# A new order of instructions for the ends of a two-layer graph kernel on one core

## The chip, the cores and the metric

The kernel runs on one core of one Trainium2 chip. The metric is the device time of one execution in microseconds (us), as the median of several runs. A profiled execution gives, besides, the span from its first to its last instruction and what each engine did in it. The engines are called PE (TensorE, matrix products), PEld (its weight loads), DVE (VectorE), ACT (ScalarE), POOL (GpSimd) and SP (SyncE, which here only issues DMAs).

## The reference

There are 128 blocks x[b] of 128 nodes by 512 features in fp32, and one 128x128 matrix adj for all of them. Two layers follow each other, each with a residual and a layer norm:

```
# layer 0, per block
A = adj @ x                       # 128x512
rm = max over features of relu(A + (A + b0 - A))  -> relu(row maximum of A + b0)
x = layernorm(x + rm)
# layer 1, per block: attention with 8 heads of 64, masked by adj == 0
q, k, v = split(x @ w_qkv)
o = (softmax(mask(q k^T / 8)) @ v) @ w_proj + b_proj
x = layernorm(x + o + layernorm(o) * gamma + beta)
```

The layer-0 line is the reference's pairwise maximum as the kernel computes it: a row maximum of adj @ x, a bias and a relu.

## The kernel before

The 128 blocks are taken in 32 groups of 4. Each group needs, per block, some 60 steps, and a step is one short function that issues a few instructions on one engine. The names of the steps are used below with the block in brackets; dm, dd, main and rest carry (group, j) instead, where j is 0 to 3 for the v product of a block and 4 to 11 for a q or k product of the whole group.

- Layer 0: load (SP) brings x; conv (PE, L633) multiplies by adj; cmax (DVE) takes the row maximum; bn and ba (DVE) or add0 and sq0 (ACT) take the moments; relu, rstdx and shiftx or rstd0 and shift0 (POOL) make scale and shift; norm0 (ACT, L705) applies them.
- The transposes of x. In group 0 tx (PE) transposes into PSUM and copy (L767) keeps a plain copy of blocks 0 and 1 for pv, a plain fp32 product with w_v (PE, L778). In every other group xpl (ACT, L717) splits x into 16-bit planes, xrow (SP, L721) writes them to DRAM, and xcross (SP) reads them back with a transposing DMA. There is one buffer of planes, so xpl of the next block waits until xrow of the last one has landed.
- The dense products are done in three reduced-precision terms. xmask, xsub (DVE, L740 and L756), xhigh and xd split x into a high part, a low part and a difference; wmask, wsub, wd, wh, wl do the same for the weights once, at the start. dm (PE, L818 and L819) does the first two terms, dd (PE, L824) the third; main (ACT, L843) and rest (DVE, L847) bring the sums to SBUF.
- Attention: S (PE, L864), masked and rmax (DVE), exps (ACT, L903), recip and wts (DVE), pln (ACT, L918), row (SP) and cross (SP), which turn the weights through DRAM as above, and AV (PE, L950). In the last group T (PE) transposes instead.
- The end of a block: omask, osub (L968), ohigh, od; po and pod (PE) multiply by w_proj; pmain, prest; res, resx, resb, reso bring the residual; sq1 to norm2 are the two layer norms; out writes the block.

The order is not written as loops. Every step of every block has a place, a number, in a table: STEADY for the groups in the middle, one period of 55.2952 apart, FIRST for groups 0 and 1, LAST for groups 30 and 31, SETUP for the weights and constants. group_plan turns the tables into a list, the list is sorted by place, and the steps are issued in that order (L1168) under a manual schedule: each engine gets its own instructions in exactly the order of the list and runs them one after the other. Only the order of the numbers matters; a number is no time. The semaphore waits follow from which step writes and reads what.

HOMES says for every tile which buffer of its kind it gets. ps_1 has four PSUM banks (0 to 3), shared by pa, ptx, pv, pm, pd, pav and the projection; ps_2 has two double ones. A step that fills a bank waits until the last reader of its former content is done. TWO says which of two engines does a step.

Of the kernel before, what the change touches and what calls it, by code (L numbers as in the profile page):

```python
# [88 lines left out]
        'load': [-901.563, -922.473, -922.478, -903.511],  # L89
        'conv': [-846.813, -915.390, -915.506, -874.949],  # L90
        'cmax': [-801.056, -837.693, -879.384, -830.372],
        'relu': [-769.981, -826.342, -869.061, -825.870],
        'bn': [-827.199, -893.843, -914.944, -858.378],
        'ba': [-823.944, -891.308, -906.541, -834.612],
        'rstdx': [-769.986, -871.005, -872.145, -809.784],
        'shiftx': [-756.335, -825.941, -839.332, -806.691],
        'norm0': [-665.371, -805.806, -813.036, -780.621],
        'tx': [-662.290, -792.690, -793.199, -771.754],
        'copy': [-659.866, -737.960],
        'pv': [-512.869, -504.297],  # L100
        'keep': [-512.082, -498.844],
        'xmask': [-660.833, -762.731, -727.868, -730.418],
        'xsub': [-655.987, -732.262, -663.602, -697.023],
        'xhigh': [-645.543, -744.320, -688.080, -657.593],
        'xd': [-624.486, -628.830, -550.270, -602.581],
        'dm': [None, None, -189.208, -190.809, -355.594, -484.251, -628.419, -495.437, -360.548, -512.270, -635.612, -488.644],
        'dd': [None, None, -190.217, -261.030, -354.973, -354.971, -354.968, -468.964, -372.501, -463.622, -459.178, -466.650],
        'main': [None, None, -144.321, -142.898, -350.075, -443.584, -557.996, -457.187, -355.005, -412.729, -587.560, -356.783],
        'rest': [None, None, -132.175, -85.246, -308.148, -283.698, -281.357, -403.261, -319.558, -356.677, -395.445, -311.676],
        'S': [-228.655, -246.003, -152.387, -143.350],  # L110
        'masked': [-207.282, -245.809, -138.500, -87.105],
        'rmax': [-204.167, -238.589, -110.297, -72.325],
        'exps': [-143.767, -228.331, -64.342, -39.835],
        'recip': [-128.447, -159.497, -59.854, -1.024],
        'wts': [-76.979, -133.784, -57.083, 1.778],
        'pln': [-56.268, -102.763, -26.594, 25.922],
        'row': [12.450, -89.665, 22.867, 38.411],
        'cross': [23.073, -54.738, 39.078, 53.987],
        'AV': [41.632, 32.084, 48.580, 62.020],
        'omask': [43.060, 38.063, 55.696, 69.240],  # L120
        'osub': [50.071, 41.766, 56.572, 73.080],
        'ohigh': [46.187, 42.319, 57.889, 94.260],
        'od': [55.963, 50.919, 66.754, 105.184],
        'po': [50.422, 45.682, 70.630, 106.044],
        'pod': [57.744, 53.653, 71.635, 105.297],
        'pmain': [53.386, 50.289, 72.129, 108.935],
        'prest': [61.548, 57.007, 81.360, 111.396],
        'res': [20.431, -449.833, 74.707, 77.734],
        'resx': [65.326, -238.611, 92.577, 103.188],
        'resb': [65.601, 62.299, 100.889, 111.137],  # L130
        'reso': [85.510, 64.948, 103.433, 114.117],
        'sq1': [69.604, 71.004, 98.646, 116.521],
        'sm1': [90.258, 64.542, 94.296, 111.885],
        'st1': [82.652, 85.464, 101.831, 117.141],
        'n1a': [90.344, 80.143, 105.417, 118.025],
        'n1b': [91.956, 89.155, 106.494, 119.198],
        'sq2': [93.227, 93.375, 115.421, 123.874],
        'sm2': [97.804, 89.471, 109.477, 120.474],
        'st2': [101.770, 106.617, 116.322, 126.682],
        'norm2': [102.343, 107.816, 117.180, 127.450],  # L140
        'out': [109.060, 121.436, 120.171, 128.392],
    },
    {
        'load': [-905.274, -696.140, -858.109, -902.178],
        'conv': [-792.111, -663.812, -712.708, -716.977],
        'cmax': [-709.318, -638.776, -690.493, -706.940],
        'relu': [-555.739, None, -616.445],
        'bn': [-703.706, -646.917],
        'ba': [-690.726, -645.927],
        'rstdx': [-558.088],  # L150
        'shiftx': [-554.898],
        'add0': [None, None, -601.344, -604.764],
        'sq0': [None, None, -567.298, -573.370],
        'rstd0': [None, None, -552.984],
        'shift0': [None, None, -518.997],
        'norm0': [-554.884, -502.496, -403.722, -417.718],
        'xpl': [-554.429, -502.196, -391.703, -416.776],
        'xrow': [-470.076, -375.192, -293.759, -319.091],
        'xcross': [-394.778, -319.316, -286.162, -305.221],
        'xmask': [-372.466, -307.177, -249.613, -262.305],  # L160
        'xsub': [-329.385, -262.572, -243.199, -244.783],
        'xhigh': [-275.237, -298.028, -199.736, -215.316],
        'xd': [-272.386, -204.299, -156.069, -159.106],
        'dm': [-10.436, 6.699, -0.683, -0.556, -143.277, -131.813, -122.870, -130.336, -39.992, -105.000, -112.136, -140.915],
        'dd': [-4.815, 6.730, 10.987, 18.045, -127.490, -108.574, -116.018, -118.700, -24.016, -29.807, -26.705, -118.919],
        'main': [1.177, 46.859, 5.350, 6.474, -132.881, -131.684, -115.120, -114.444, -37.456, -88.207, -40.875, -105.235],
        'rest': [1.965, 48.653, 18.540, 20.009, -121.662, -87.519, -102.746, -111.824, -17.484, -23.344, -19.627, -52.332],
        'S': [-11.079, -17.443, -16.256, -1.509],
        'masked': [-10.554, -17.005, -9.812, 6.626],
        'rmax': [-5.380, -16.675, 5.417, 19.372],  # L170
        'exps': [-2.148, -10.618, 7.233, 22.858],
        'recip': [0.765, -9.571, 18.704, 35.680],
        'wts': [6.167, -4.226, 43.122, 35.837],
        'pln': [6.770, 3.285, 56.604, 44.172],
        'row': [16.487, 7.371, 56.843, 54.372],
        'cross': [20.475, 25.543, 61.651, 64.066],
        'AV': [52.512, 52.150, 68.373, 68.094],
        'omask': [63.494, 57.640, 72.391, 77.549],
        'osub': [65.657, 58.241, 79.421, 99.342],
        'ohigh': [65.260, 57.805, 75.915, 100.961],  # L180
        'od': [73.704, 59.905, 88.130, 103.708],
        'po': [69.517, 61.895, 86.954, 104.135],
        'pod': [76.042, 63.614, 93.677, 111.272],
        'pmain': [74.426, 66.789, 96.190, 114.037],
        'prest': [78.300, 68.797, 99.841, 114.042],
        'res': [60.118, 65.341, 97.902, 93.885],
        'resx': [69.088, 68.611, 98.642, 103.374],
        'resb': [72.493, 73.045, 103.649, 115.231],
        'reso': [89.889, 83.803, 109.798, 129.413],
        'sq1': [81.258, 68.947, 107.075, 118.043],  # L190
        'sm1': [86.719, 87.045, 108.620, 116.281],
        'st1': [92.581, 80.193, 119.323, 125.369],
        'n1a': [91.249, 88.810, 118.652, 131.743],
        'n1b': [92.613, 88.815, 123.900, 132.261],
        'sq2': [96.351, 99.085, 124.215, 132.381],
        'sm2': [97.859, 94.858, 125.503, 145.539],
        'st2': [103.342, 102.489, 128.234, 147.699],
        'norm2': [106.369, 103.393, 130.775, 147.977],
        'out': [115.175, 111.613, 147.933, 149.596],
# [28 lines left out]
        'S': [28.905, 28.062, 51.236, 50.349],  # L228
        'masked': [35.272, 37.129, 54.944, 52.529],
        'rmax': [38.080, 38.174, 96.293, 53.051],  # L230
        'exps': [43.345, 51.622, 115.258, 64.145],
        'recip': [49.538, 54.728, 141.791, 70.564],
        'wts': [52.585, 60.636, 147.678, 82.495],
        'pln': [53.581, 61.741, 154.283, 105.933],
        'row': [56.112, 76.901, 159.668, 153.223],
        'cross': [81.989, 84.562, 182.868, 153.372],
        'AV': [85.872, 91.909, 188.022, 153.844],
        'omask': [106.182, 104.214, 188.234, 161.077],
        'osub': [154.777, 106.177, 189.068, 161.598],
        'ohigh': [152.931, 109.298, 193.692, 166.063],  # L240
        'od': [160.331, 144.311, 199.215, 178.233],
# [955 lines left out]
```

## Time and profile before

| | |
|---|---|
| time, median of 3 runs | 1821.26 us (1821.16 to 1822.58) |
| the profiled execution's own time | 1820.26 us |
| its span, first to last instruction | 1818.5 us |
| matrix products on PE | 10525, busy 1791.8 us |
| DVE / ACT / POOL busy | 1584.7 / 1543.2 / 1246.7 us |
| granted TensorE clock, mean | 0.997 |
| DMA | 303.94 MB, of 16 engines the main queue takes 62.9% |

PE has one program, so its idle time can be listed gap by gap from its timeline. In us from the start of the span:

| PE starts again at | idle before it | instruction |
|---|---|---|
| 3.74 | 3.74 | adjT_ps, waits for adj |
| 4.57 | 0.38 | first conv |
| 11.20 | 0.52 | tx(1) |
| 13.79 | 1.94 | tx(3) |
| 16.12 | 0.81 | tx(0) |
| 18.47 | 1.72 | conv(7) |
| 102.74 | 0.95 | dm(1,2) |
| 163.96, 172.02, 177.77, 179.16 | 0.14, 0.17, 0.06, 0.29 | groups 2 and 3 |
| 234.95 | 1.83 | conv(21) |
| 280 to 1680, 8 places | 0.03 to 0.80 each | |
| after the last product, at 1807.7 | 10.8 | the last block's layer norms and its output |

A line of the profile's groups, waits or timeline has the start, the length, the engine, the source line, the operation, what it writes and reads, and in brackets the idle time of the engine just before it with what ended that idle time. "issue" stands where the profile shows nothing that was waited for. Ends of matmuls are modelled; the distance from one start to the next is the better measure (0.227 us for a 128x512 product of the reduced kind).

### The profile page before, as it was taken

How to read it: one execution, taken by the hardware profiler on the slowest of the kernel's cores; microseconds unless marked ns; L12 is line 12 of the kernel's file. 1: busy time of each engine (PE TensorE's matmuls, PEld its weight loads, DVE VectorE, ACT ScalarE, POOL GpSimd, SP SyncE). 2: the span in 40 equal slices, each digit the busy share in tenths (PEclk: the TensorE clock that was granted, in tenths of full speed). 3: DMA queues.
4: the chain of work that ended last, by engine and by line, in shares of the span. 5: the costliest groups of instructions: out<-in, count | busy, mean ns of one | idle time of the engine just before them, and what ended most of it. 6: DMA issues, size and time to landing. Idle time of an engine off the chain costs nothing.

```text
span 1818.5 us, 32498 instructions
## 1 busy us (share of the span) xinstructions
PE 1791.8 (99%) x10525; PEld 1428.0 (79%) x10525; DVE 1584.7 (87%) x2575; ACT 1543.2 (85%) x3959; POOL 1246.7 (69%) x1892
## 2 busy tenths in 40 slices
PE   7999999999999999999999999999999999999997
PEld 4777878888887878887888888888878878877885
DVE  7988888988888988889888888888888988889887
ACT  6987888888888888888889888888888888888786
POOL 5256577666776767776667867667766678668867
PEclk9999999999999999999999999999999999999999
DMA  5666666666666676665767655766567766567543
GB/s 154 159 149 173 161 176 160 155 186 184 161 171 156 168 190 167 183 165 155 186 180 169 162 171 159 198 164 184 163 148 184 180 173 184 154 167 186 169 133 99
DMA packets 486714, 303.94 MB, mean 167 GB/s; under 512 B 399504, under 2 KB 403728, under 8 KB 486544
## 3 DMA queue, kind: packets, MB, share of 16 engines
q1 hardware_dynamic: 485680, 300.75, 62.9%
q8 instruction: 83, 1.36, 0.3%
q10 hardware_dynamic: 864, 1.12, 0.2%
q14 instruction: 87, 0.71, 0.1%
HBM read 73.20 MB, written 131.07 MB: 112 GB/s over the span
## 4 chain that ended last, share of the span: by engine, by line
PE 89%; ACT 5%; DVE 2%; DMA 2%; POOL 1%; issue 1%; SPq 0%; ACTq 0%; POOLq 0%; DVEq 0%
PE psc L864 7%; PE pav L950 6%; PE pa L633 5%; ACT e L903 1%; ACT squares L1063 1%; DMA rows<-planes 1%; ACT planes L918 1%; DMA eT<-rows 1%; DMA rowsx<-xplanes 1%; ACT xplanes L717 0%; PE pv L778 0%; ACT qkT L843 0%; ACT o L1105 0%; POOL sum L1069 0%; ACT xt L705 0%
## 5 line engine op out<-in xcount | busy, mean ns | idle before, releaser
L903 ACT ACTIVATE e<-e,nmax 128x128 f32<-128x128 f32 x1016 | 392.7, 393 | 4.6 <-DVE nmax L886 4.6
L918 ACT COPY planes<-e 128x2048 uint16<-128x2048 uint16 x124 | 235.3, 1897 | 63.3 <-DMA rows<-planes 39.9
L1069 POOL TENSOR_TENSOR sum<-sum,mhalf 128x1 f32<-128x1 f32 (+1 forms) x287 | 195.8, 682 | 23.9
L1063 ACT ACTIVATE squares<-o,sum 128x512 uint8<-128x512 f32 x256 | 182.6, 715 | 18.3 <-DVE o L1056 14.9
L903 ACT ACTIVATION_READ_ACCUMULATOR e<-e,nmax 128x1 f32 x1016 | 195.9, 193 | 0.0
L1072 POOL TENSOR_SCALAR sum<-sum 128x1 f32<-128x1 f32 x256 | 74.9, 294 | 172.3 <-DVE o L1056 169.1
L912 DVE TENSOR_TENSOR e<-e,sums 128x1024 f32<-128x1024 f32 x128 | 182.8, 1445 | 1.9
L1053 POOL TENSOR_TENSOR xb<-xb,o 128x512 f32<-128x512 f32 x124 | 176.7, 1434 | 9.5 <-DVE o L1056 4.9
L1068 POOL TENSOR_SCALAR sum<-sum 128x1 f32<-128x1 f32 (+1 forms) x287 | 103.3, 360 | 114.7 <-ACT squares L1063 96.9
L1044 POOL TENSOR_TENSOR xb<-xb,beta_sb 128x512 f32<-128x512 f32 x124 | 162.7, 1312 | 7.3
L717 ACT COPY xplanes<-xt 128x1024 uint16<-128x1024 uint16 x124 | 129.3, 1043 | 41.1 <-DMA rowsx<-xplanes 40.9
L878 DVE SCALAR_TENSOR_TENSOR e<-psc,mask 128x1024 f32<-128x1024 f32 x127 | 152.0, 1217 | 1.0 <-PE psc L864 0.8
L886 DVE TENSOR_REDUCE nmax<-e 128x8 f32<-128x1024 f32 x127 | 150.9, 1206 | 0.1
L750 POOL TENSOR_TENSOR x_d<-x_h,x_l 128x512 fp32r<-128x512 f32 x97 | 129.2, 1333 | 14.0 <-DVE x_l L756 5.6
L864 PEld LDWEIGHTS psc<-qkT 64*128 64x128 f32 x2048 | 119.5, 188 | 18.3 <-issue 15.3
L864 PE MATMUL psc<-qkT 64*128 64x128 f32 x2048 | 132.1, 279 | 0.0
L633 PE MATMUL pa<-xt,adjT 128*128 128x512 f32 x256 | 125.2, 608 | 4.0 <-DVE ol L968 1.8
L950 PE MATMUL pav<-eT,v 128*64 128x128 f32 x2048 | 126.7, 276 | 1.1 <-DMA eT<-rows 1.1
L950 PEld LDWEIGHTS pav<-eT,v 128*64 128x64 f32 x2048 | 110.5, 137 | 18.2 <-issue 12.7
L1105 ACT ACTIVATE o<-o,sum 128x512 f32<-128x512 f32 x128 | 103.7, 810 | 9.5 <-POOL sum L1101 9.4
L649 POOL TENSOR_SCALAR rm<-rm,b_sb 128x2 f32<-128x2 f32 (+1 forms) x66 | 21.5, 326 | 131.4 <-DVE rm L644 130.9
L1084 DVE SCALAR_TENSOR_TENSOR o<-o,sum,gamma_sb 128x512 f32<-128x512 f32 x128 | 102.8, 803 | 9.3 <-POOL sum L1072 4.9
(4264 smaller groups left out, 5596.6 us busy)
## 6 DMA issues: line engine op xcount, KB each, us to landing
rows<-planes SPq DMA_DIRECT2D x124, 512.0 KB, 4.1
xt<-in_x_dram SPq DMA_DIRECT2D x128, 256.0 KB, 3.4
xb<-in_x_dram SPq DMA_DIRECT2D x128, 256.0 KB, 3.7
out_dram<-o SPq DMA_DIRECT2D x128, 256.0 KB, 2.8
rowsx<-xplanes SPq DMA_DIRECT2D x124, 256.0 KB, 3.4
wraw<-in_L_gnn_w_qkv_dram SPq DMA_DIRECT2D x8, 256.0 KB, 3.9
xT<-rowsx SPq DMA_TRANSPOSE x124, 3.7
eT<-rows SPq DMA_TRANSPOSE x124, 4.6
```

The source lines that it names most:

```text
L633: nc.tensor.matmul(pa[b], adjT, xs[b], start=True, stop=True)
L864: nc.tensor.matmul(psc[:, s, hp, :], qkT[hs, hp, i, :], qkT[hs, KC + hp, i, :], start=not with_mask, stop=not with_mask or hp == HP - 1,)
L878: nc.vector.scalar_tensor_tensor(es[b], pscs.pop(b).rearrange("p s a m -> p (s a) m"), scale, mask_b, op0=ALU.mult, op1=ALU.add,)
L886: nc.vector.tensor_reduce(nmaxs[b], es[b], AX.X, ALU.max, negate=True)
L903: nc.scalar.activation(es[b][:, j, :], src[:, j, :], AF.Exp, bias=nmax[:, j : j + 1], scale=by, accum_out=sums[b][:, j : j + 1],)
L912: nc.vector.tensor_tensor(es[b], es[b], sums.pop(b)[:, :, None].to_broadcast([P, H, P]), op=ALU.mult,)
L918: nc.scalar.copy(pl, es.pop(b).rearrange("p h m -> p (h m)").bitcast(U16).rearrange("p (m s) -> p s m", s=2),)
L950: nc.tensor.matmul(pavs[b][s * HD : (s + 1) * HD, hp, :], v[:, h * HD : (h + 1) * HD], eT[:, s * HP + hp, :], start=True, stop=True,)
L1044: nc.gpsimd.tensor_tensor(xbs[b], xbs[b], beta_sb, op=ALU.add)
L1053: engine.tensor_tensor(xbs[b], xbs[b], os[b], op=ALU.add)
L1063: nc.scalar.activation(junk[:, turn[0], :], src, AF.Square, bias=s[:, 0:1], scale=-float(D), accum_out=s[:, 1:2],)
L1069: nc.gpsimd.tensor_tensor(s, s, mhalf[:, :n], op=ALU.pow)
```

## The change

Only the tables FIRST, LAST, SETUP and HOMES are changed; the code, STEADY and TWO are the same. Every number of FIRST and of SETUP is new, and many of LAST. Since a number acts only through the order, the change is best read as the order on each engine that comes out:

| engine | steps | whose position differs | from | to |
|---|---|---|---|---|
| PE | 1411 | 82 | the 4th | the 154th (pod(7)) |
| ACT | 1657 | 165 | the 2nd | the 225th |
| DVE | 2317 | 234 | the 5th | the 305th, and one more pair |
| POOL | 1273 | 101 | the 2nd | the 130th |
| SP | 899 | 78 | the 3rd | the 116th |

The one pair near the end of DVE is osub(123) and n1b(121), which change places. Nothing else of the last two groups is in another order. After some 240 us of the time before, all engines have the old order.

The first steps, before and after:

```
PE   before adjT conv(2) conv(1) conv(3) conv(0) tx(2) tx(1) tx(3) conv(4) tx(0) conv(7) conv(6) dm(0,10) dm(0,6) conv(5) pv(0) dm(0,9) pv(1) dm(0,7)
     after  adjT conv(2) conv(1) conv(0) conv(3) tx(2) tx(1) tx(3) conv(7) tx(0) conv(6) conv(4) dm(0,10) dm(0,6) conv(5) pv(1) pv(0) dm(0,11) dm(0,7)
DVE  before adjc bn(2) ba(2) bn(1) ba(1) cmax(2) bn(3) wmask6 mask cmax(1) ba(3) cmax(3) bn(0) wsub6 ba(0) wmask10 wd6 cmax(0) xmask(1) wsub10 xsub(1) wd10 xmask(3) xmask(2) xsub(3) xsub(2) xmask(0) copy(0) xsub(0)
     after  adjc bn(2) ba(2) bn(1) cmax(2) bn(0) ba(1) mask bn(3) cmax(1) ba(0) ba(3) wmask6 cmax(0) cmax(3) wsub6 wmask10 wd6 wsub10 xmask(1) wd10 xsub(1) xmask(2) xmask(3) xsub(2) xsub(3) cmax(7) xmask(0) xsub(0)
ACT  before norm0(2) wh6 norm0(1) wl6 norm0(3) xhigh(1) wh10 copy(1) norm0(0) xhigh(3) wl10 xhigh(0) main(0,10) wh9 wl9 main(0,6)
     after  norm0(2) norm0(1) wl6 wh6 wh10 norm0(3) copy(1) xhigh(1) wl10 norm0(0) xhigh(3) xhigh(0) add0(6) main(0,10) sq0(6) wl11 add0(7) wh11 main(0,6)
SP   before load(2) load(1) load(3) lw6 load(0) lw10 lw9 load(4) load(7) load(6) lw11 load(5) lw7
     after  load(2) load(1) load(0) load(3) lw6 lw10 lw5 load(7) lw11 load(6) load(4) lw9 gammb load(5) lw7
```

Further on, around the first attention blocks:

```
PE   before AV(1) S(5) S(6) AV(0) S(4) dm(1,0) po(1) AV(2) po(0) dd(1,0) pod(1) S(7) dm(1,2) dm(1,3) pod(0)
     after  AV(1) S(5) AV(0) S(4) S(6) dm(1,0) dd(1,3) po(1) dm(1,3) dd(1,0) pod(1) S(7) AV(2) dd(1,2) po(0) pod(0) conv(14) conv(15) dm(1,1) dm(1,2)
ACT  before xpl(8) ohigh(1) wl12 exps(5) xpl(9) ohigh(0) norm0(10) exps(4) xpl(10) main(1,0)
     after  xpl(8) pln(3) ohigh(1) xpl(9) main(1,0) exps(5) main(1,3) norm0(10) ohigh(0) xpl(10) exps(4)
SP   before row(1) lw13 cross(1) load(11) load(10) row(0) load(8) load(9) res(0) row(2) cross(0) gamma row(3) cross(2) xrow(8) xcross(8) load(15) xrow(9) cross(3) xcross(9) load(14) xrow(10)
     after  row(1) res(0) load(11) load(10) load(8) row(0) load(9) cross(0) cross(1) row(2) gamma cross(2) xrow(8) row(3) xcross(8) load(15) xrow(9) xcross(9) load(14) xrow(10) cross(3)
```

The core of the diff that makes these orders, cut to lines that are spoken of:

```diff
 FIRST = [
     {
-        'xsub': [-655.987, -732.262, -663.602, -697.023],
-        'copy': [-659.866, -737.960],
+        'xsub': [-1083.930, -1180.700, -1122.347, -1118.864],
+        'copy': [-1043.146, -1134.306],
...
     {
-        'main': [1.177, 46.859, 5.350, 6.474, -132.881, -131.684, -115.120, -114.444, -37.456, -88.207, -40.875, -105.235],
+        'main': [-9.238, 11.669, 15.115, -8.754, -191.405, -120.492, -50.145, -169.927, -37.891, -64.302, -288.051, -67.751],
...
 LAST = {
-        'osub': [154.777, 106.177, 189.068, 161.598],
+        'osub': [106.122, 95.757, 123.487, 111.452],
-        'n1b': [187.418, 162.789, 248.823, 206.581],
+        'n1b': [121.574, 110.635, 139.436, 129.404],
...
 HOMES = {
-    'wr': '10--020122100112',
+    'wr': '10--020011102011',
```

In HOMES the long runs of the middle keep their pattern and change the numbers of the buffers (1 and 2 or 3 trade names); the first few places of each row are new. The transposed blocks of group 0 keep their PSUM banks ('ptx': '2213').

## The prediction

> **What bounds the kernel now.** I read the page's busy shares, slices and chain first.
>
> ```profile
> PE 1791.8 (99%) x10525; PEld 1428.0 (79%) x10525; DVE 1584.7 (87%) x2575; ACT 1543.2 (85%) x3959; POOL 1246.7 (69%) x1892
> ...
> PE   7999999999999999999999999999999999999997
> ...
> PE 89%; ACT 5%; DVE 2%; DMA 2%; POOL 1%; issue 1%; SPq 0%; ACTq 0%; POOLq 0%; DVEq 0%
> ```
>
> PE works without a break except in the first and the last slice. The change adds and removes no instruction, so it can only move PE's idle time, 1818.5 - 1791.8 = 26.7 us, and time that PE spends at a low clock. Next the busy time by stretches:
>
> ```profile
> 0.00:20.00 20.00, 10.88 (x30) 5.09 (x31) 13.90 (x29) 8.85 (x14) 10.59 (x32) 0.97 0.70 202
> ...
> 40.00:100.00 60.00, 60.00 (x370) 48.01 (x369) 57.33 (x89) 56.97 (x157) 11.98 (x17) 1.00 0.62 161
> 100.00:150.00 50.00, 49.05 (x278) 38.66 (x278) 39.52 (x65) 38.93 (x85) 32.32 (x47) 1.00 0.62 153
> ...
> 200.00:250.00 50.00, 48.17 (x296) 38.18 (x295) 46.16 (x68) 41.47 (x115) 32.50 (x46) 1.00 0.56 153
> ...
> 1800.00:1818.50 18.50, 7.69 (x28) 3.35 (x24) 9.38 (x20) 10.26 (x21) 12.52 (x27) 0.79 0.19 72
> ```
>
> The first number is the length, then PE, PEld, DVE, ACT, POOL. Of the 26.7 us, 9.1 lie before 20 us, 10.8 after the last product, and 6.8 between. From 20 to 100 us PE has no gap, though DVE and ACT are nearly full too. Then PE's timeline at the start:
>
> ```profile
> 13.79 0.66 PE L711 MATMUL ptx<-ident,xt 128*128 128x128 f32 x4 [1.94 <-ACT xt L705]
> 14.29 1.02 PE L633 MATMUL pa<-xt,adjT 128*128 128x512 f32 x2
> 16.12 0.63 PE L711 MATMUL ptx<-ident,xt 128*128 128x128 f32 x4 [0.81 <-DVE x_l L756]
> 18.47 3.43 PE L633 MATMUL pa<-xt,adjT 128*128 128x512 f32 x4 [1.72 <-issue]
> 20.91 1.42 PE L818 MATMUL pm_(0, 10)_264<-x_h,w_h 128*128 128x512 f32 x1
> ```
>
> Two conv take 3.43 us at 18.47, 1.72 each, against 0.86 for one elsewhere (14.29 to 15.15). Dense work, dm(0,10), begins only behind them. The clock view:
>
> ```profile
> 15.40:18.80 3.40, 0.96 (x5) 0.71 (x6) 3.40 (x6) 1.71 (x3) 0.94 (x1) 1.00 0.87 245
> 18.80:22.20 3.40, 3.40 (x6) 1.39 (x5) 3.40 (x7) 0.63 (x1) 3.17 (x4) 0.50 0.62 181
> ```
>
> After 3.4 us with only 0.96 us of PE work the granted clock is 0.50 for the next 3.4 us. DVE, with its order, is what PE waits for here; and DVE itself waits once:
>
> ```profile
> 15.28 0.69 DVE L756 TENSOR_TENSOR x_l<-ptx,xm 128x512 fp32r<-128x512 f32 x1 [1.18 <-ACT xraw L772]
> ```
>
> That is xsub(1) waiting for copy(1) on ACT, which reads the same PSUM bank. Last, the chain around PE's one gap near 100 us:
>
> ```profile
> 94.85 0.94 ACT xplanes L717
> ...
> 96.21 4.86 DMA rowsx<-xplanes
> ...
> 101.15 1.05 ACT xplanes L717
> 102.19 0.50 ACT v L843
> ...
> 102.74 0.50 PE pm_(1, 2)_1078 L818
> ```
>
> main(1,0) stands on ACT behind xpl(10), which waits for the DMA that empties the one plane buffer; dm(1,2) needs main(1,0)'s bank. 0.95 us of PE are lost.
>
> [...]
>
> **The change part by part.** The sum is made against the profiled execution: its own time 1820.26 us, span 1818.5 and 1.76 around it. The median of the runs is 1.0 above it; I carry differences over to the median.
>
> The tail (groups 30 and 31): PE, ACT, POOL and SP keep their order, DVE swaps osub(123) and n1b(121), 0.6 us apart; PE has no gap between 1700 and 1800 us to show a wait there. I take 0; bounds 0.7 either way, one such instruction. The 10.8 us after the last product stay.
>
> The start, DVE. It runs as before up to cmax(2) at 6.69. From there to xsub(1) the new list has 17 instructions, cmax(2) the first: eleven at 0.60 us start to start, two weight masks at 0.33, three small bn results at 0.09 and the mask at 0.17, in sum 7.7: xsub(1) at 14.4, end 15.1. tx(1), at about 11.8, is in time (norm0(1) is 0.6 later than its 10.33, since its POOL steps now stand behind shiftx(2)). Now copy(1) waits for xsub(1), not the reverse. So ACT, free at 14.2, does copy(1) to 15.65, xhigh(1) to 16.25, wl10 and norm0(0) to 17.55; tx(0) at 17.6 to 18.1. On DVE xmask(3) needs the buffer that xhigh(1) reads: it starts at 16.25 and loses 0.65 where 1.18 was lost; then xsub(2), xsub(3), cmax(7), xmask(0), xsub(0) at 0.60 each: end 19.95, against 20.76. copy(0) now runs after it. PE: conv(6) and conv(4) follow tx(0), 18.1 to 19.85 at full clock; their banks are free at 17.5 and 18.1 (xsub(2), xsub(3)); load(6) is issued at 13.1, behind lw11, which needs wd6's end at 12.7, and takes 3.2: 16.3. dm(0,10) starts at 20.0 and ends 8 x 0.227 later, 21.8; before, dm(0,6) took its place at 23.77. Gain 1.95. The clock decides: the window 15.4 to 18.8 would hold 1.4 us of PE work, between the 0.96 that lost it and the 1.52 that kept it. If lost, conv(4) takes 1.7 and dm(0,10) ends about 23.3: gain 0.45. I take 1.9.
>
> What covers the rest of the start: copy(0) is wanted by pv(0), at 28, and done at 24.5. The last two w_v loads move behind xhigh(0): issued by 20.4, landed by 23.3 at 2.9 each, wanted at 24.5. load(5) is on SP behind lw9 and gammb: issued 18.2, landed 22, wanted 23.6. keep(0) on ACT, behind xpl(5) and its DMA, is the tightest, done at about 39.3 by the durations above for dd(0,7) at 39.5. Each costs what it is late, if it is; I take 0.
>
> The gap at 102.74: main(1,0) now stands before exps(5), exps(4) and xpl(10), and dm(1,2) comes seven steps later; cross(3) is issued after xrow(10). I take all of 0.95; bounds 0 and 0.95.
>
> The four small gaps at 164 to 179 us, 0.66 together: order around them changes; I take 0.3, bounds 0 and 0.66. S(7) and AV(2) now follow each other; AV(2) alone cost PE 0.09 before it and 0.12 after it (95.75 and 96.78 against a start distance of 0.227): 0.2.
>
> The gap at 234.95:
>
> ```profile
> PE pa L633 <- DVE ol L968: 1.8, 1, 1.8
> ```
>
> DVE runs without idle from prest(9) at 220.2, released by pod(9) on PE, to osub(10). The new order has the same instructions between them, and PE has the same distance from pod(9) to conv(21). So the gap moves along: 0; bounds -1.0 and +1.8, since od and xd took 1.35 and 1.74 there where 0.68 is usual.
>
> Sum: 1.9 + 0.95 + 0.3 + 0.2 = 3.35. Profiled 1816.9; median 1821.26 - 3.35 = 1817.9.
>
> **Rivals.** (1) The clock: PE falls to half clock anyway. 0.45 in place of 1.9: gain 1.9, 1819.4. For it: 1.4 us in the window is borderline[...]. Against: 1.52 was enough. (2) More goes: the 1.83 at 234.95 and all of the small gaps: 3.35 + 1.83 + 0.36 = 5.5, 1815.7. For it: DVE idles 3.0 us before 198.6, and pmain(7), prest(7) are moved up into it. (3) The change does nothing at the start, since every chain there is re-dealt but of the same length: 1821.3. (4) Slower: cross(1) was issued at 69.19, before row(0) had been; now it stands behind row(0) and cross(0) on SP, and AV(1), still PE's first, waits for it. row(0) at 72.8 lands after 3.0, cross(0) holds SP for 2.6, cross(1) starts about 78.5 and lands after 4.5 to 7.7 (the four transposes of group 0): 83 to 86.2. AV(1) is wanted at 86.77 - 1.9 = 84.9, so mostly covered. If pln(0) isn't earlier than before, 1.9 more: 88.1, a stall of 3.2; xrow(8), further back on the same queue, is late by as much, and with it xpl(9) and main(1,0): another 2.2 on dm(1,3). 5.4 - 3.35 = +2.05: 1823.3. It ends slower from a landing of 88.2 on. Against: pln(0) is the 16th ACT step from exps(1) in both orders, and exps(1) is released by PE.
>
> **How the numbers follow.** Forecast 0.46 (1816.9 to 1819.0 by its bounds), clock 0.19, more 0.17, nothing 0.06, slower 0.12. A change of 0.2%, 3.64 us, about what a measurement can tell from none, lies at 1817.62 and 1824.9. Faster: all of (2) and 0.43 of the forecast, 0.17 + 0.20 = 0.37. Slower: half of (4), 0.06. Same: 0.57. The range 1815.5 to 1821.6 leaves out most of (4) and the lower half of (2).
>
> **What would show it.** Right: dm(0,10) starting near 20.0 with no stretch at 0.50 after 12 us; DVE's wait for copy(1) gone and a shorter one before xmask(3); no gap at the q, k and v products of group 1; the gap before conv(21) still there. Wrong: a second stretch at half clock; PE waiting for a transpose at AV(1), or for ACT at dd(0,7); SP's cross(1) landing after 86; any new gap in the tail, where nothing should differ.

## The result and the profile after

| | before | after |
|---|---|---|
| median of 20 runs each | 1821.85 us (1819.40 to 1826.08) | 1818.85 us (1815.89 to 1821.61) |
| ratio after / before | | 0.9981, 95% interval 0.9975 to 0.9988 |
| the profiled execution's own time, span | 1820.26, 1818.5 | 1821.09, 1819.3 |

The ratio is a gain of 3.5 us, between 2.2 and 4.6; the two medians of the table lie 3.0 apart. The forecast was 3.35. The profiled execution of after is one of its longer ones, 2.2 us above its median, and that of before lies 1.6 under its own, so the two spans can't be subtracted; stretches within them can. The busy shares and the chain of after:

```profile
PE 1792.0 (98%) x10525; PEld 1428.6 (79%) x10525; DVE 1580.8 (87%) x2575; ACT 1543.3 (85%) x3959; POOL 1248.8 (69%) x1892
...
PE 90%; ACT 3%; DMA 2%; DVE 2%; POOL 1%; issue 1%; POOLq 0%; DVEq 0%; ACTq 0%
```

PE is still the bound, with the same busy time. To place the difference I cut PE's timeline at two of its conv records that both kernels have in the same place in the order: A, the 21st (two records make one conv; 82.19 us in before) and B, the 51st (269.24). This gives three stretches, and a table for every kernel of this study. "Half" is the time at a granted clock of 0.50 in the profile, the tail apart.

| kernel | first product | first product to A | half before A | A to B | PE idle in A to B | B to last product | PE idle in it |
|---|---|---|---|---|---|---|---|
| before | 3.74 | 78.45 | 3.41 | 187.05 | 3.44 | 1538.44 | 3.30 |
| after | 4.13 | 78.95 | 6.83 | 184.87 | 1.72 | 1540.52 | 5.24 |
| e1 main early (before) | 4.05 | 78.76 | 3.41 | 187.71 | 3.63 | 1539.45 | 3.98 |
| e2 power early (after) | 4.08 | 79.74 | 6.83 | 185.37 | 2.15 | 1536.93 | 2.13 |
| e3 fill (after) | 4.07 | 77.67 | 0 | 183.92 | 1.24 | 1537.84 | 2.69 |
| e4 power and fill (after) | 3.54 | 79.51 | 3.41 | 184.59 | 1.66 | 1540.51 | 4.83 |
| e5 late order only | 4.04 | 78.25 | 0 | 184.79 | 1.55 | 1538.13 | 3.17 |
| e6 early order only | 3.54 | 77.38 | 3.41 | 194.48 | 7.48 | 1537.66 | 2.81 |
| e7 fill (before) | 4.09 | 78.20 | 0 | 186.11 | 2.51 | 1539.24 | 3.29 |
| e8 chain on DVE, fill (after) | 4.08 | 79.76 | 3.41 | 183.43 | 0.98 | 1538.25 | 2.66 |
| e9 early order only, again | 3.67 | 78.78 | 6.83 | 188.73 | 4.36 | 1539.79 | 4.22 |
| e10 reso(7) early (before) | 4.09 | 78.94 | 3.41 | 187.11 | 3.52 | 1539.51 | 4.12 |
| e11 reso(7) late (after) | 3.49 | 79.29 | 6.83 | 184.68 | 1.61 | 1539.06 | 3.73 |
| e12 start and fill (after) | 3.85 | 77.71 | 0 | 183.41 | 0.97 | 1539.47 | 4.02 |

Read by columns. From B on, PE's work without its idle time is 1534.8 to 1536.0 us in every kernel; what differs there is 2.1 to 5.2 us of idle time, which the profiles put mostly to waits for POOL (the statistics of the layer norms) and DVE, and in part to transposing DMAs (1.3, 0.7 and 1.1 us in before, 2.1, 2.6 and 0.5 in after). Its mean is 3.7 us in the four kernels with before's order throughout (before, e1, e7, e10) and 3.6 in the eight with after's late part, so it isn't the change's. From A to B the order of before takes 186.1 to 187.7 and that of after 183.4 to 185.4, the joined kernels e6 and e9 aside. Up to A after is not shorter than before, it is 0.50 longer in these two profiles. After the last product come 10.76 us in before and 10.80 in after.

So the gain is not where most of it was forecast. The start of after by PE's timeline:

```profile
12.10 0.66 PE L711 MATMUL ptx<-ident,xt 128*128 128x128 f32 x4 [1.25 <-ACT xt L705]
16.55 1.11 PE L711 MATMUL ptx<-ident,xt 128*128 128x128 f32 x4 [3.79 <-ACT xt L705]
...
22.41 0.80 PE L818 MATMUL pm_(0, 10)_278<-x_h,w_h 128*128 128x512 f32 x1
```

The second line is tx(3), at 16.55 where the forecast had it by 14.3, behind 3.79 us of idle time; dm(0,10) starts at 22.4, not 20.0. The windows, cut at the edges of the clock's records (length, PE, PEld, DVE, ACT, POOL, granted clock):

```profile
11.95:15.36 3.41, 0.66 (x4) 0.42 (x4) 3.41 (x8) 1.77 (x4) 3.25 (x4) 1.00 0.64 175
15.36:18.77 3.41, 2.22 (x6) 1.25 (x6) 1.60 (x3) 3.08 (x6) 3.00 (x9) 0.50 0.16 60
18.77:22.18 3.41, 3.41 (x8) 2.03 (x8) 3.07 (x6) 1.10 (x2) 0.31 (x1) 0.50 0.81 269
```

After a window with 0.66 us of products the clock is 0.50 for two windows, one more than in before. There the window at this place had 1.52 us, and the one behind it, which the prediction shows, was at 1.00:

```profile
12.00:15.40 3.40, 1.52 (x6) 0.69 (x6) 2.22 (x5) 2.47 (x5) 2.60 (x9) 1.00 0.78 240
```

tx(3) waits for norm0(3) on ACT, and that for POOL. POOL's timeline of after, with rstdx(3)'s power instruction and relu(3):

```profile
11.46 2.52 POOL L691 TENSOR_TENSOR sum<-sum,mhalf 128x1 f32<-128x1 f32 x1
13.98 0.86 POOL L649 TENSOR_SCALAR rm<-rm,b_sb 128x1 f32<-128x1 f32 x1
```

and DVE's timeline beside it:

```profile
11.33 0.68 DVE L599 TENSOR_TENSOR wraw<-wraw,wh 128x512 f32<-128x512 f32 x1
...
12.87 0.69 DVE L599 TENSOR_TENSOR wraw<-wraw,wh 128x512 f32<-128x512 f32 x1
...
17.76 0.69 DVE L740 TENSOR_SCALAR xm<-ptx 128x512 int32<-128x512 int32 x1 [1.81 <-PE ptx L711]
```

The power instruction takes 0.57 elsewhere at the start and 0.92 in before. Here it ran 2.52, while DVE did wsub6, wmask10, wd6 and wsub10 back to back, 11.33 to 13.55; relu(3) behind it took 0.86 in place of 0.29, beside wd10. The price comes at the end: xmask(3) on DVE waits 1.81 us for tx(3), more than the 1.18 us that it lost in before at copy(1).

What PE waits for between 90 and 240 us in after:

```profile
PE pm_('o', 7)_2095 L818 <- ACT oh L746: 0.9, 1, 0.9
PE psc L864 <- DVE e L878: 0.4, 1, 0.4
PE pa L633 <- ACT qkT L843: 0.4, 1, 0.4
```

The gap at 102.74 is gone and so are the four small ones (0.66). conv(21), the third line, waits 0.39 for ACT where it waited 1.83 for DVE's osub(10). Two gaps are new: po(7), 0.91, and an S product, 0.42 (the lines round to 0.9 and 0.4). In sum 0.95 + 0.66 + 1.44 - 0.91 - 0.42 = 1.72 us less idle time, and 0.46 less in which PE was busy.

### The profile page after: what moved, and what is told of

Its sections match the earlier page's. It is cut to its first block, busy times and chain, and to the rows that moved or that the text cites. A ratio compares the mean times of both kernels' runs of the same rounds, so it can differ in the third digit from the quotient of the medians.

```text
span 1819.3 us, 32504 instructions
## 1 busy us (share of the span) xinstructions
PE 1792.0 (98%) x10525; PEld 1428.6 (79%) x10525; DVE 1580.8 (87%) x2575; ACT 1543.3 (85%) x3959; POOL 1248.8 (69%) x1892
## 4 chain that ended last, share of the span: by engine, by line
PE 90%; ACT 3%; DMA 2%; DVE 2%; POOL 1%; issue 1%; POOLq 0%; DVEq 0%; ACTq 0%
PE psc L864 7%; PE pav L950 6%; PE pa L633 6%; DMA rows<-planes 1%; ACT e L903 1%; ACT squares L1063 1%; ACT planes L918 1%; PE pv L778 0%; DMA out_dram<-o 0%; ACT qkT L843 0%; DMA xt<-in_x_dram 0%; DMA eT<-rows 0%; DVE o L1056 0%; ACT xplanes L717 0%; POOL sum L1069 0%
## 5 line engine op out<-in xcount | busy, mean ns | idle before, releaser
L912 DVE TENSOR_TENSOR e<-e,sums 128x1024 f32<-128x1024 f32 x128 | 183.4, 1450 | 1.8
L705 ACT ACTIVATE xt<-xt,sum 128x512 f32<-128x512 f32 x128 | 100.9, 811 | 11.1 <-POOL sum L699 11.1
```

What stands on the lines that cost most here:

```text
L912: nc.vector.tensor_tensor(es[b], es[b], sums.pop(b)[:, :, None].to_broadcast([P, H, P]), op=ALU.mult,)
```

## The experiments

Each ratio is to runs of before that were taken on the same chip with it, since the median of before itself was 1820.5 to 1823.0 us on the three chips.

### e1: only main(1,0) moved, in before

```diff
-        'main': [1.177, 46.859, 5.350, 6.474, -132.881, ...
+        'main': [-0.6, 46.859, 5.350, 6.474, -132.881, ...
```

> The order of before, with one step moved: main(1,0) on ACT stands ahead of xpl(10), so it no longer waits for the DMA that empties the plane buffer. If the gap of 0.95 us at 102.74 is a plain loss: the gap goes, dm(1,2) follows S(7) at 101.8, and the time is 0.95 us under before. Rival, the lost time is given back at the next late step (dm(1,3) or a transpose): a new gap of about the same size before 125 us, and the time of before within 0.3 us.

Measured: ratio 0.9996 (0.9988 to 1.0004). The waits of PE from 100 to 180 us:

```profile
PE pa L633 <- DMA xt<-in_x_dram: 0.7, 1, 0.7
PE pp_('o', 4)_1781 L824 <- DVE o L1017: 0.5, 1, 0.5
```

The gap at dm(1,2) is gone, but a conv at 107.88 now waits 0.69 us for its load, and the step at 173.4 0.51 in place of 0.17. A to B took 187.71, no less than before's 187.05. In the profile this is the rival: the loss moved to the next late transfer, load(14), which landed at 107.74. The times can't decide it, since the interval holds both no gain and one of 0.95 us. In after the same move goes with loads that stand earlier on SP (load(14) ahead of cross(3)), and no such wait is there. The gap was not a fixed size either: it is 0.31 in e10 and absent in e7, both in before's order at that place, and e10's A to B took 187.11 all the same.

### e2, e3, e4: what holds the start of after

e2 takes the power instruction out from under DVE's run:

```diff
-        'relu': [-1177.028, -1358.334, -1365.432, -1207.842],
+        'relu': [-1177.028, -1328.3, -1365.432, -1207.842],
-        'rstdx': [-1176.421, -1358.529, -1446.494, -1211.102],
-        'shiftx': [-1127.315, -1355.468, -1363.585, -1177.210],
+        'rstdx': [-1176.421, -1358.529, -1446.494, -1328.4],
+        'shiftx': [-1127.315, -1328.2, -1363.585, -1177.210],
```

> The order of after, with rstdx(3) on POOL ahead of relu(1) and shiftx(1), so that its power instruction runs while DVE reads PSUM (cmax), not while DVE subtracts two SBUF operands (wsub6, wd6, wsub10). If those DVE instructions held it up: the power instruction takes 0.57 to 0.9 us in place of 2.5, norm0(3) starts at 13.3 to 13.8 in place of 15.7, tx(3) near 14.3, dm(0,10) between 20.0 and 21.5 in place of 22.8, and the time is 1.3 to 2.5 us under after. Rival A, the long instruction is of another cause: it stays near 2.5 us wherever it stands, nothing gained. Rival B, [...]norm0(1) and tx(1) come at 13 or later, xmask(1) with them, and half of the gain or more is lost.

e3 adds products on PE where it is idle:

```diff
+    def fill(n):
+        t = ps_2.tile([P, P], FP, tag="ps2_0", bufs=1, name=f"fill_{n}")
+        for _ in range(n % 100):
+            nc.tensor.matmul(t, adjT, adjT, start=True, stop=True)
+
+    for u, n in ((-1244.4, 5), (-1238.3, 112), (-1161.1, 204)):
+        at(u, fill, n)
```

> The order of after, with 21 products of adjT with itself (128x128, about 0.21 us each) added on PE into a bank that nothing uses yet: 5 behind tx(2), 12 behind tx(1), 4 behind conv(7), where PE is idle. Their result is read by nobody. If the half clock at the start is a cost of its own: no record at 0.50 before the tail, tx(3) at its old 16.5, conv and transposes of 16 to 22 us at half their time, dm(0,10) near 21.3 in place of 22.8, and the time 1.2 to 2 us under after. Rival, DVE alone sets the start and the clock is hidden behind it: dm(0,10) and the time within 0.3 us of after.

e4 is e2 with `((-1244.4, 8), (-1238.3, 104), (-1161.1, 204))`.

> Both edits on after: rstdx(3) early on POOL, and 16 added products on PE (8 behind tx(2), 4 behind tx(1), 4 behind conv(7)). If the two costs are separate and both real: full clock throughout, norm0(3) near 13.5, dm(0,10) near 20.0 as it was forecast for after, and the time 2.5 to 3 us under after, near 1816. Rival, once DVE is no longer held up its own 17 instructions set the end and the clock is covered: as with the early power instruction alone.

Measured: e2 0.9984 (0.9978 to 0.9991), e3 0.9969 (0.9958 to 0.9980), e4 0.9988 (0.9982 to 0.9995). POOL's timeline of e2 gives the answer on the slow instruction:

```profile
10.32 0.56 POOL L691 TENSOR_TENSOR sum<-sum,mhalf 128x1 f32<-128x1 f32 x1
...
11.26 2.29 POOL L697 TENSOR_TENSOR sum<-sum,rm 128x1 f32<-128x1 f32 x1
```

rstdx(3), moved, takes 0.56. The long one is now the first instruction of shiftx(1), an addition on one column, 0.19 elsewhere: 2.29 us, from 11.26 to 13.55, and DVE's run lasts from 11.28 to 13.50. So it isn't the power operation; what POOL starts as this run begins is held, in both of these profiles until the run ends or just past it: to 13.98 in after, where the run's last instruction ends at 13.55, and to 13.55 in e2. That is rival B of e2: norm0(1) and tx(1) come late (tx(1) at 14.99, where it was 12.10), and the start is longer, 79.74. In these two profiles no POOL instruction ends between the four of the run (in e6, e8 and e12, below, one did, after 1.03 to 1.10 us). Why POOL is held isn't shown. In before the same four DVE instructions stood further apart, with ba(0), cmax(0) and xmask(1) among them, and three POOL instructions beside them took 0.35, 0.46 and 0.25 us more than elsewhere (0.92, 0.65 and 0.54, where 0.57, 0.19 and 0.29 are usual).

The clock is a cost of its own: in e3 the start is 1.3 us shorter than in after. The windows of e3:

```profile
11.58:14.99 3.41, 3.14 (x29) 2.96 (x28) 3.41 (x7) 2.07 (x4) 3.33 (x3) 1.00 0.49 151
14.99:18.40 3.41, 2.30 (x16) 1.64 (x15) 1.84 (x4) 2.79 (x5) 2.92 (x10) 1.00 0.32 94
```

With products in the gaps no record is at 0.50; tx(3) stays at 16.48, and dm(0,10) starts at 21.34 as expected. The start takes 77.67, where after's takes 78.95. All six runs of e3 have the same mean clock, 0.998. Of the 20 runs of after, five have 0.998 (mean 1816.97 us), four 0.997 (1818.65) and eleven 0.996 (1819.50), so by estimate the start falls to half clock in most executions, as in the profile: before the tail the profiles have no window at 0.50 in e3 (mean clock 0.998), one in before (0.997) and two in after (0.996). How much of these 2.5 us is the clock's own isn't shown: in e11, which has the same start, six runs at 0.998 and six at 0.996 differ by 0.9 us in the mean. Against after's own ratio e3 is 0.0012 lower, but the intervals touch. In e4 tx(1) came late, at 14.45, its fill ended before that, and one window, 3.41 us, was at 0.50: half of the repair undid the other.

### e5, e6, e9: after's order in one part only

The two orders have the same set of steps up to a place near 90 us on each engine. e5 takes the order of before up to there and that of after from there on; e6 and e9 are the reverse:

```diff
-    plan.sort(key=lambda p: p[:2])
+    rank = {n: k for k, n in enumerate(EARLY)}
+    first = lambda p: rank.get(" ".join([p[2].__name__, *map(str, p[3])]), len(rank))
+    plan.sort(key=lambda p: (first(p), *p[:2]))
```

EARLY is the list of the first 378 steps (372 in e9) in the one order; the tables are those of the other. HOMES follows the order of each part, with the buffers of the second part renamed so that what lives across the joint keeps its place.

> The order of before for the first 378 steps (all engines, up to some 90 us: PE to dm(1,0), ACT to ohigh(1), DVE to masked(6), POOL to od(1), SP to load(15)), then the order of after. From the two traces: between the 20th and the 50th conv product before takes 187.05 us and after 184.87. If after's gain lies in groups 1 to 4 alone: that stretch takes 184.9 here too, the start is as before, and the time is 2.2 us under before (ratio 0.9988), with no gap at 102.74 and about 0.4 in place of 1.83 before conv(21). Rival, the gain hangs on the start: 0 to 0.5 us under before.

> The reverse: the order of after for the same 378 steps, then that of before. If after's start gains nothing: the time of before within 0.8 us[...], and the gaps of before come back, 0.95 near 102 us and 1.83 before conv(21). Rival, the start gains 1.9 as it was forecast: 1.9 us under before (ratio 0.9990). Second rival: the gap at 102.74 depends on when the transposes of group 2 come, so it isn't back at its size.

> The order of after for the first 372 steps, then that of before, joined a little earlier than in the last such kernel (DVE at masked(5), POOL at rstd0(10)), so that rmax(5) and exps(5) keep the place that ohigh(0) and po(0) need in the order of before. Expected if the start of after gains little by itself: no gap of 3.3 us at 99, the way from the first product to the 20th conv between 77.4 and 79.0 us (before 78.45), the gaps of before back (0.95 near 102, 1.83 before conv(21)), and the time within 1 us of before (ratio 0.9994 to 1.0004). Rival, the start gains 1.9 us: ratio 0.9990 or below.

Measured: e5 0.9986 (0.9979 to 0.9994); e6 1.0032 (1.0021 to 1.0044); e9 1.0015 (1.0007 to 1.0023).

e5 did what was expected: A to B in 184.79, no gap at 102.74, 0.39 before conv(21), and a gain of 2.5 us (1.1 to 3.8). After's order and buffers from 90 us on carry 2.5 of the 3.5 us by these figures, though the interval is wide.

e6 as a whole can't be read as a test of the start. Its joint left exps(5) on ACT waiting for a late rmax(5), with ohigh(0) behind it, and PE stood for 3.3 us at po(0); behind that come two windows at 0.50:

```profile
94.05:97.46 3.41, 1.53 (x19) 0.94 (x17) 0.76 (x3) 3.29 (x17) 0.00 (x0) 1.00 0.08 15
97.46:100.88 3.42, 2.00 (x5) 1.55 (x6) 3.42 (x5) 3.42 (x10) 0.00 (x0) 0.50 0.38 129
100.88:104.29 3.41, 3.41 (x10) 2.64 (x9) 2.45 (x5) 3.24 (x13) 2.71 (x2) 0.50 1.08 93
```

The first stretch of e6 can be read, though. With after's order in it, it took 77.38, 1.07 less than in before, and still has one window at half clock. POOL shows why (this kernel's line numbers are others; the first is rstdx(3)'s power instruction, the second relu(3)):

```profile
10.87 1.10 POOL L1026 TENSOR_TENSOR sum<-sum,mhalf 128x1 f32<-128x1 f32 x1
11.96 1.20 POOL L984 TENSOR_SCALAR rm<-rm,b_sb 128x1 f32<-128x1 f32 x1
```

The power instruction took 1.10, not 2.52. It ended at 11.97, near the end of wmask10 (11.88), and relu(3) was then held to 13.16, the end of DVE's run being at 13.08. Counted from the first product, tx(3) came at 11.70 and dm(0,10) at 16.72, where after has 12.42 and 18.28. The same order on POOL and DVE thus gives two outcomes: 2.52 in the profiles of after, e3, e9 and e11, 1.10 in e6 and 1.06 in e12. What decides between them isn't shown.

e9, joined elsewhere, still has 0.45 us at that po(0) and 0.67 at a dd of group 3, new ones, beside 1.82 before conv(21); its start took 78.78. In its profile the power instruction took 2.52 and two windows were at half clock, as in after. The rival of 1.9 us is out: this start gives nothing in that profile, and the kernel as a whole, with before's order behind the joint, is 2.7 us slower (1.3 to 4.2). The two parts don't add: 1.0015 x 0.9986 = 1.0001, and both together are 0.9981.

### e7: products for the clock in before

```diff
+    for u, n in ((-792.6, 8), (-736.8, 104), (-662.2, 207)):
+        at(u, fill, n)
```

> The order of before, with 19 products of adjT with itself added on PE where it is idle: 8 behind tx(1), 4 behind conv(4), 7 behind tx(0); nobody reads them. If the half clock costs before as well: no record at 0.50 before the tail, conv(7) and conv(6) 0.86 us each in place of 1.72, dm(0,10) ending near 22.1 to 22.6 in place of 23.77, and the time 1.2 to 1.7 us under before. Rival, DVE sets the start of before (xsub(0) ends at 20.76): under 0.5 us.

Measured: 0.9995 (0.9987 to 1.0003). No record at 0.50, but dm(0,10) starts at 21.93, and PE waits 0.50 us for DVE's xsub(0) there; dm(0,10) ends at 23.86, as late as without the products (23.77). The start takes 78.20, 0.25 less. In the profile this is the rival: in before DVE sets the start and hides the half clock (0.25 us without it), in after it doesn't (1.3 in e3). The interval alone would allow the 1.2 us expected, but the runs of before speak for the rival too: of the 51 taken with e1 to e4, thirty have a clock of 0.997 (mean 1820.40 us) and ten 0.998 (1820.26).

### e8 and e12: two attempts at a better start

e8 is e2 with the last two POOL steps of block 3 (relu's one instruction and shiftx's three) on DVE, norm0(3) earlier on ACT, and `((-1244.4, 9), (-1161.1, 205), (-1111.5, 303))` as fill:

```diff
-        'relu': [-1177.028, -1358.334, -1365.432, -1207.842],
+        'relu': [-1177.028, -1328.3, -1365.432, -1260.3],
-        'shiftx': [-1127.315, -1355.468, -1363.585, -1177.210],
+        'shiftx': [-1127.315, -1328.2, -1363.585, -1260.2],
-        'norm0': [-1124.016, -1263.817, -1342.860, -1162.887],
+        'norm0': [-1124.016, -1263.817, -1342.860, -1224.9],
...
-        nc.gpsimd.tensor_scalar(r, r, b0_sb, 0.0, op0=ALU.add, op1=ALU.max)
+        engine = nc.vector if b == 3 else nc.gpsimd
+        engine.tensor_scalar(r, r, b0_sb, 0.0, op0=ALU.add, op1=ALU.max)
...
-        nc.gpsimd.tensor_tensor(both, mean, r, op=ALU.add)
+        engine = nc.vector if b == 3 else nc.gpsimd
+        engine.tensor_tensor(both, mean, r, op=ALU.add)
...
```

> The order of after with rstdx(3) early on POOL; relu(3) and shiftx(3), four instructions on one column each, on DVE behind cmax(3), so that no short chain of POOL lies under wsub6 to wsub10; norm0(3) on ACT ahead of wl6, wh6 and wh10; and 17 added products on PE (9 behind tx(2), 5 behind conv(7), 3 behind tx(0)) for the clock. If the DVE run of two-operand SBUF instructions and the clock were what kept after's start from its forecast: shiftx(1) on POOL at its usual 0.27 us an instruction, norm0(1) near 12.0, tx(3) near 13.6, DVE without idle to xsub(0), which ends near 19.8, dm(0,10) near 19.9, no record at 0.50 before the tail, and the time 1.2 to 1.6 us under the order of after with added products alone (ratio to before near 0.9962). Rival, the start isn't on the path behind dm(0,6): dm(0,10) early, and the time within 0.5 us of that run (0.9969).

e12 leaves POOL as it is and re-deals the other engines around the wait that stays:

```diff
-        'copy': [-1043.146, -1134.306],
+        'copy': [-1043.146, -1170.0],
-        'xsub': [-1083.930, -1180.700, -1122.347, -1118.864],
-        'xhigh': [-1064.032, -1132.498, -1082.389, -1074.587],
+        'xsub': [-1083.930, -1180.700, -1126.0, -1118.864],
+        'xhigh': [-1064.032, -1175.0, -1082.389, -1074.587],
...
-        'conv': [-1161.040, -1024.186, -1166.330, -1216.399],
+        'conv': [-1161.040, -1024.186, -1166.995, -1216.399],
+    for u, n in ((-1244.4, 5), (-1238.3, 112)):
+        at(u, fill, n)
```

> The order of after with 17 added products on PE for the clock (5 behind tx(2), 12 behind tx(1)), and its start re-dealt around the wait that stays under full clock, DVE's 1.6 us for xhigh(1) ahead of xmask(3): on ACT xhigh(1) and copy(1) ahead of norm0(3), on DVE xsub(2) ahead of xmask(3), on PE conv(6) ahead of tx(0). Expected: DVE's wait down to 0.3 to 0.8 us (now for tx(3)), xsub(0) ending near 20.3 in place of 21.26, dm(0,10) near 20.3 in place of 21.34, no record at 0.50 before the tail, and the time 0.5 to 1.1 us under the order of after with added products alone: ratio to before near 0.9965. Rival, what comes behind dm(0,6) (weights, transposes, the product with w_v) takes the gain back: ratio 0.997.

Measured: e8 0.9994 (0.9986 to 1.0003), e12 0.9974 (0.9963 to 0.9984).

In e8 the first half came as expected: shiftx(1) on POOL at 0.27 an instruction, norm0(1) at 12.0, tx(3) at 13.6. Then norm0(0) still stood on ACT behind copy(1), which waits for xsub(1) (16.5): tx(0) came at 18.98 behind 2.75 us of idle PE. POOL was held at rstdx(0) instead (1.03 and 0.91 us). A window went to half clock (3.41 us at 0.50), and my own fill behind tx(0) ran in it at 0.21 us a record, 1.3 us on the path. The start took 79.76. Of the expectation only its first links held.

In e12 POOL's power instruction took 1.06, but norm0(3) stands behind copy(1) on ACT and began at 15.73. DVE's wait is 0.88, now for tx(3), xsub(0) ends at 20.93 in place of 21.26, and the next thing is there at once:

```profile
20.33 1.10 PE L633 MATMUL pa<-xt,adjT 128*128 128x512 f32 x2 [0.92 <-DVE xm L740]
```

conv(4) waits 0.92 us. The profile names DVE's xmask, long done; load(4) landed at 20.19, issued at 17.33. So dm(0,10) starts at 21.01 instead of 20.3, and the way to A is 77.71, as in e3 (77.67): the rival in its number, 0.997, though most of the loss came before dm(0,6), at this load. e3 and e12 have the lowest ratios here, with e11 (0.9975) beside them; none is separated from after by its interval. All runs of e3 and e12 have a mean clock of 0.998.

### e10 and e11: reso(7) and the gap before conv(21)

```diff
-        'reso': [89.889, 83.803, 109.798, 129.413],
+        'reso': [89.889, 83.803, 109.798, 119.405],
```

e11 goes the other way, in after:

```diff
-        'reso': [90.775, 78.049, 121.462, 123.654],
+        'reso': [90.775, 78.049, 121.462, 129.413],
```

> The order of before with one step moved on POOL: reso(7), whose inputs are there, goes ahead of shift0(18) and relu(22), in place of between st2(6) and xd(19). In before it ran at 225.71 beside od(8) on DVE, which took 1.35 us in place of 0.68, and pushed xd(19), resb(9) and xd(17) on POOL behind it. If DVE and POOL slow each other[...]: od(8) back near 0.68, DVE's way from prest(9) to osub(10) (14.0 us) shorter by 0.7 to 2.0, the gap before conv(21) at 0 to 1.1 us in place of 1.83, and the time 0.7 to 1.8 us under before. Rival, the collisions only move to other pairs: the gap within 0.3 us of 1.83.

> The order of after with reso(7) on POOL put back to its number in before, between st2(6) and st1(7), so that it runs at about 227.8, beside rmax(15), n1a(7) or n1b(7) on DVE. If it was this move that freed DVE: the gap before conv(21), 0.39 in after, is 1.0 to 2.0 us, and the time 0.6 to 1.6 us over after. Rival, the earlier n1a(6), n1a(7) and prest(7) on DVE made the gain: the gap within 0.3 us of 0.39.

Measured: e10 0.9998 (0.9990 to 1.0006), e11 0.9975 (0.9968 to 0.9983). The thought was that DVE's slow instructions in before, two of them

```profile
226.21 1.35 DVE L750 TENSOR_TENSOR od<-oh,ol 128x512 fp32r<-128x512 f32 x1
...
232.56 1.74 DVE L750 TENSOR_TENSOR x_d<-x_h,x_l 128x512 fp32r<-128x512 f32 x1
```

made osub(10) late, and that after had freed them. Beside od on DVE (226.21 to 227.56) POOL did reso(7) and xd(19), 1.30 and 1.74 us from 225.71 on; beside xd (232.56 to 234.30) two more 128x512 additions or subtractions, 1.71 us each from 232.03 on, where x_d alone took 1.29 at 222.79. In e10 reso(7) was out of the way, xd(19) took its place on POOL (226.59, 1.29 us), and DVE was as slow as before:

```profile
227.09 1.34 DVE L750 TENSOR_TENSOR od<-oh,ol 128x512 fp32r<-128x512 f32 x1
```

The gap was 1.84, so the rival. In e11 it was 0.39, unchanged, though DVE's way from prest(9) to osub(10) was 13.6 us, near before's 14.0 (12.65 in after). So reso(7)'s place is worth 0.95 us on DVE's way there, and yet conv(21) started at 233.02, before osub(10) did (233.32): it doesn't wait for osub(10) any more. The tables say why: in before conv(21) gets bank 2 of ps_1 behind AV(10), which omask(10) and osub(10) empty; in after AV(10) has bank 3, and bank 2 comes from dm(4,7), which main(4,7) on ACT empties. The line "PE pa <- ACT qkT" shown above is this wait. The gap before conv(21) is 1.82 to 1.85 in all five profiles with before's homes there beside its own (e1, e6, e7, e9, e10), and 0.39 in all eight with after's.

The bank is not all of it. osub(10) and conv(21) in before, then in after:

```profile
234.22 0.68 DVE L968 TENSOR_TENSOR ol<-pav,oxh 128x512 fp32r<-128x512 f32 x1
234.95 1.13 PE L633 MATMUL pa<-xt,adjT 128*128 128x512 f32 x2 [1.83 <-DVE ol L968]
...
233.04 0.68 DVE L968 TENSOR_TENSOR ol<-pav,oxh 128x512 fp32r<-128x512 f32 x1
233.69 1.12 PE L633 MATMUL pa<-xt,adjT 128*128 128x512 f32 x2 [0.39 <-ACT qkT L843]
```

In before conv(21) starts 0.05 us behind osub(10)'s end. In after osub(10) ends at 233.73. Had conv(21) still waited for it, it would have started near 233.78: a gap of 0.48, by estimate from these lines, in place of 0.39. So in after the shorter way on DVE was enough. In e11, where osub(10) ended at 234.00, the same estimate gives 1.42, and there the new bank saved 1.0. Nor would the bank alone have helped in before's order: main(4,7) ended there at 235.15, later than osub(10). Both parts of the change thus act on this gap, the order and the buffers. A run with this one home changed was not made.

## Why the prediction was right, point by point

The time was right: 3.35 us forecast, 3.5 (2.2 to 4.6) measured, just within 0.2%. That the sum fits is luck in the main: of its 3.35 us, 1.9 were put where the profile of after shows nothing gained, and 1.44 came from a gap that was put at 0. Two wrong terms have opposite signs.

| term | forecast | in the two profiles | what the runs showed |
|---|---|---|---|
| tail | 0 | 0.04 longer | 10.78 to 10.80 us in the eight with after's late part, 10.76 to 11.05 in the others: right |
| start | 1.9 | -0.5 | 0.8 with no window at 0.50 (e3), 1.1 with POOL held for less (e6); wrong in after's profile |
| gap at 102.74 | 0.95 | 0.95 | gone in after; taken away alone it brought nothing in e1's profile |
| four small gaps | 0.3 | 0.66 | mis-sized |
| gap before conv(21) | 0 | 1.44 | wrong: DVE's way is 1.35 shorter, and another bank (e11) |
| new gaps in groups 1 to 4 | none | -1.33 | not foreseen |
| S(7) and AV(2) in a row | 0.2 | | PE's busy time from A to B is 0.46 less; its parts weren't measured |

The start. "So ACT, free at 14.2, does copy(1) to 15.65" failed. norm0(3) stood ahead of copy(1) on ACT, and I had it done at 14.2 without costing the five POOL instructions that it waits for beside DVE's new run: the first two took 2.52 and 0.86 us. They ended at 15.65 and norm0(3) began at 15.69, so copy(1) came at 16.4, and xmask(3) lost 1.81 in place of the forecast 0.65. The 17 instructions on DVE came as forecast (xsub(1) at 14.67, with the first product 0.39 later), and the wait of xsub(1) for copy(1) did go. The late tx(3) then also left PE idle for most of a clock window: the forecast said that 1.4 us of products in 15.4 to 18.8 would decide, but the half clock came already behind the window before, 11.95 to 15.36 with 0.66. Nor is it likely, by estimate from e10, that 1.4 us would have kept the clock: a window with 1.45 was followed by half clock there. So rival (1), half clock anyway, came in most runs (eleven of 20 at 0.996, four at 0.997), and rival (3), nothing at the start, is nearest to the profile. Neither gave its total, since groups 1 to 4 gave more.

The gap before conv(21). "The new order has the same instructions between them ... So the gap moves along: 0" failed. The instructions are the same, but the sum took over the 14.0 us that they took in before. In after the way was 12.65: od and xd, beside other instructions of POOL, took 0.68 and 0.67 in place of 1.35 and 1.74, the very pair that the forecast gave as its reason for the bound of +1.8. It also compared the orders and not HOMES, though the front of this text says that the first places of each row are new. This is the extra of rival (2), 1.83 forecast for it and 1.44 measured, with another cause than the one given.

The gap at 102.74 was worth its 0.95 in these profiles, but in e1's profile taking it away alone gave nothing, and in e7 and e10 its size was another without a change of order there. I took one profile's size for the price.

The slower rival (4) did not come. cross(1), behind row(0) and cross(0) on SP, was issued at 80.6 and landed at 85.2, in the forecast range of 83 to 86.2, and AV(1) had no wait before it.

The gain of 3.5 us, put together from the profiles: A to B takes 187.0 in the mean of the four profiles with before's order and homes throughout (before, e1, e7, e10) and 184.4 in the eight with after's late part, 2.6 less; some of these carry an edit of their own. The way to A took 77.4 to 77.7 where no window was at 0.50 or POOL was held for less (e3, e12, e6), 0.7 to 1.1 less than in before, and 78.8 to 79.3 otherwise (after, e9, e11), 0.3 to 0.8 more; how often each comes in the runs of after isn't known. 2.6 and a little more or less is inside the interval. How the remaining 0.9 is split isn't settled, since the idle time from B on swings by 3 us.

## What to carry to other kernels

When an order is re-dealt, check the buffers as well as the steps: for each gap, look up which tile's former content the waiting instruction replaces, in both tables, and how late that tile's last reader is in each order. When DVE instructions like wsub6, wmask10, wd6 and wsub10 are drawn together, list what POOL has to do in that stretch, small instructions included (one took 2.52 us in place of 0.57 here), and ask who waits for it. And price a gap of one profile by several: here one was 0.95, 0.31 or absent in the same order, another 1.82 to 1.85 every time.

## What the runs showed of the hardware

- Beside four DVE instructions in a row a one-column instruction on POOL took 2.52 us in after, e3, e9 and e11, where 0.57 is usual, and another 2.29 in e2, where 0.19 is. In e6, e8 and e12 the first one took 1.10, 1.03 and 1.06; the next took 1.20 in e6 and 0.91 in e8.
- At the start PE's busy time in a clock window of 3.41 us and the clock of the next window were, from full clock: 0.66 us and 0.50 (after), 0.96 and 0.50 (before), 1.45 and 0.50 (e10), 1.52 and 1.00 (before), 2.30 and 1.00 (e3); further on, 1.53 and 0.50 (e6). From half clock: 2.00 and 0.50 (e6), 2.22 and 0.50 (after), and with PE busy throughout 1.00 (before and after). The ends of matmuls are modelled, so the second digit is soft. The window of e10:

```profile
16.71:20.12 3.41, 1.45 (x6) 0.90 (x7) 3.41 (x7) 1.23 (x3) 1.43 (x1) 1.00 0.82 228
```

- With products that nobody reads in PE's idle time, all six runs of e3 and all eight of e12 have a mean clock of 0.998. The way to A was 1.3 us shorter with them where PE was on the path (e3 against after), and 0.25 where DVE was (e7 against before). Added products in a half-clock window took 0.21 us a record (e8), against 0.11 at full clock (e3).
